# The liquid state divided by DT * DT in a decoder layer woven by a planner

## The chip, the cores and the metric

The kernel runs on one core of a Trainium2 chip, in one launch. Its engines work in parallel, each through its own queue in program order: TensorE (matmuls and transposes, into eight PSUM banks), VectorE, ScalarE (activations), GpSimd (POOL in the profile) and SyncE (SP), which issues the DMAs. They wait for one another through semaphores. The metric is the device time of the launch in microseconds, lower is better.

## The reference

The input is 2 x 1024 tokens of 256 features, and the layer adds three parts to it in turn: causal attention with a liquid cell and a feed-forward net, cross attention to 77 context tokens, and eight parallel trees of 255 nodes. The change touches the liquid cell:

```
b, s, d = x.shape
...
x = x + attn
ctx = attn.reshape(b * s, d)
xs = _ln(x, g1, b1).reshape(b * s, d)
vs = jnp.zeros_like(xs)

def step(carry, _):
    xs, vs = carry
    u = jnp.tanh(ctx @ w_ctx + xs @ w_x + b_inl)
    vn = vs + DT * (u - xs - vs)
    xn_ = xs + DT * vn
    return ((xn_, vn), None)
(xs, vs), _ = jax.lax.scan(step, (xs, vs), None, length=NUM_ITERS)
x = x + xs.reshape(b, s, d)
```

There are eight steps and DT is 0.1.

## The kernel before, in words

The tokens are cut into NTB = 4 blocks of TB = 512, two for each batch. Each block goes through chains of work written as Python generators: `scores` (first norm, queries, keys, values, the rows' maxima), `values` (exponentials and the weighted sums), `opening` (output projection, sum `h0`), `middle` (the liquid cell, the feed-forward net, cross attention, the last norm) and `leaves` (the trees). They run for different blocks at the same time.

**Who sets the order.** A planner, the class `Clock`, weaves these chains while the program is being built. A chain yields what it needs next: an operation (`Op`) with an engine, a cost and its operands; a set of tiles that must be ready for a matmul, with a number of free PSUM banks; or a condition. `weave` (L354) asks every chain for the earliest time at which it can go on by the planner's own costs, adds what going on is worth (a change of TensorE's kind of matmul counts 0.135 to 0.215 in `TURNS`, L99), and takes the least, in tenths of a microsecond; ties go to the chain that is most behind its due time. If a chain yields a list of operations, the planner takes the one that ends first by its costs; in this way a copy out of PSUM goes to ScalarE or VectorE (`evict`, L167). `beside` (L343) sends a piece of work off as a chain of its own and gives back a condition that it is over. The result is one fixed order for each engine; a different cost or one more operation anywhere can give another order from there on. Matmuls come in three kinds: on the full array, on 32 rows (scores of one head; up to four heads go side by side), and into 32 columns (`p,v`). In the profile nearly all planned instructions have the lines of the planner's helpers (L165 matmul, L181 transpose, L197 ScalarE, L207 VectorE, L216 and L218 GpSimd), so groups are told apart by tiles.

**The liquid cell** (`liquid`, L965) keeps features on the partitions: 2 halves (`c`) of 128 partitions by 512 tokens. Two PSUM banks `ps` hold the argument of the tanh for all eight steps and are only added to. With w the velocity over DT, a step is: tanh of `ps` plus `b_ac` into `w` on ScalarE, once per half; `w` plus the remainder `r` on VectorE (in the first step minus `xs`); the matmuls `w_dx` by `w`, where `w_dx` is `w_x` times DT * DT, into `ps`; then on VectorE, for each half, the state `xs = w * DT * DT + xs` and the remainder `r = w * (1 - DT) - xs`. The first matmuls of a block are `w_x` by `xs`. In the profile `xs` is the tile `xn_l`, because the norm that makes it names it so. At the end `add_tokens_first` transposes `xs` and `add_half` (L652) adds it to `h0` (`h` in the profile).

**Buffers.** Tiles of the middle chain and of the startup come from one ring of six buffers of the same size, with the tag `d`; the seventh tile takes the buffer of an earlier one and has to wait until that one's readers are through. At the start the ring is filled by the loads of `woT`, `w_ctx`, `ctxT`, `xwk`, `xwv` and by the tile `mask32` (L511), which GpSimd fills with the causal mask (a memset and a select). `w_x` (L497) has a buffer of its own.

**The startup.** GpSimd's order is: identity, `mask32`, the constant `half`, then the powers with which the norms take their inverse roots. VectorE's order is: clearing of `qT` and two `nmax`, the cast of `mask32` to `mask` and of the identity, ones for the values, and then the statistics of the first block `xn`, the normalized `xc`. TensorE's order is: `w_ctx` by `woT` (the chain `prepare`, L1198), the first context keys (`ctxT` by `xwk`), the transposes of `xc`, more context keys, the queries. SP issues the loads in the order of the program.

Of the kernel before, what the change touches and what calls it, by code (L numbers as in the profile page):

```python
# [26 lines left out]
DC = D // P  # L27
VROW = H * (HD + 1) + SLOT - HD - 1
FF = 1024
NITER, DT = 8, 0.1  # L30
# [8 lines left out]
_COLS = {}  # L39
# [375 lines left out]
def decoder_kernel(ctx: ExitStack, tc: tile.TileContext, ins: dict, out: bass.AP):  # L415
# [8 lines left out]
    const = ctx.enter_context(tc.tile_pool(name="const", bufs=1))  # L424
# [3 lines left out]
    clock = Clock(nc)  # L428
# [6 lines left out]
    def bank():  # L435
        return banks(1)[0]
# [5 lines left out]
    def dtile(name, shape=(P, DC, TB)):  # L442

        return work.tile(list(shape), F32, tag="d", name=name, bufs=6)


    def load(name, shape, pool=const, tag=None, **kw):
        t = pool.tile([P, *shape], F32, tag=tag or name, name=name + "_sb", **kw)
        flat = t if len(shape) == 1 else t.rearrange("p a b -> p (a b)")
        clock.load(flat, ins[name])  # L450
        return t
# [28 lines left out]
    vecs = load("vecs", (NCOLS,))  # L480
    x0 = load_x(0, "xn")
    d = dict(pool=work, tag="d", bufs=6)
# [11 lines left out]
    xrow = work.tile([P, D], F32, tag="raw", name="xrow", bufs=2)  # L494
    clock.load(xrow, ins["vrows"][0:1, 4 * D :].to_broadcast([P, D]))
    wo = load("wo", (DC, D))
    w_x = load("w_x", (DC, D))  # L497
    xwq = load("xwq", (DC, D))
    xwo = load("xwo", (DC, D))
    paths32 = load("paths", (2, P), pool=work, tag="raw", bufs=2)  # L500
# [1 line left out]
    def col(name, i):  # L502
        at = _COLS[name][0] + i
        return vecs[:, at : at + 1]
# [12 lines left out]

    paths = const.tile([P, 2, P], BF16, tag="paths16", name="paths16")
    w_dx = const.tile([P, DC, D], F32, tag="w_dx", name="w_dx")
    half_b = const.tile([P, 2 * PAR], F32, tag="half_b", name="half_b")  # L520


# [38 lines left out]
    def fill_late():  # L561
        for t in (qT[1], xq, *nmax[2:]):
            yield zeros(t)
        yield clock.vector("tensor_copy", paths, paths32)
        yield clock.activation(w_dx, w_x, AF.Copy, scale=DT * DT)
        for name in ("ff", "trees"):
            for w in streams[name]:
                w.more()
                w.more()
        at = _COLS["b_in"][0]  # L570
        yield clock.vector("tensor_scalar", half_b, vecs[:, at : at + 2 * PAR], 0.5, None, ALU.mult)
        spare.extend(nmax[2:])
        done.add("filled late")
# [37 lines left out]
    def scaled(dst, src, mv, rstd):  # L611

        for i in range(NQ):
# [2 lines left out]
                ALU.subtract, ALU.mult,  # L616
            )

    def evicted(ops, *banks):
        yield ops  # L620
        clock.free(*banks)

    def features_first(dst, src, name, g=None, b=None):

        made = []
        for c in range(DC):
            yield (src,), 1
            ps = bank()
            for i in range(NQ):
                clock.transpose(  # L630
                    ps[:, i * P : (i + 1) * P], src[:, i, c * P : (c + 1) * P], ident
                )
            affine = () if g is None else (col(g, c), col(b, c))
            made.append(clock.beside(evicted(clock.evict(dst[:, c, :], ps, *affine), ps)))
        yield (), lambda: all(m() for m in made)

    def add_tokens_first(dst, src, name):

        made = []
        for j in range(2):  # L640
            yield (src,), 1
            ps = bank()
            for i in range(2):
                for c in range(DC):
                    cols = slice((2 * j + i) * P, (2 * j + i + 1) * P)
                    clock.transpose(
                        ps[:, i * D + c * P : i * D + (c + 1) * P], src[:, c, cols], ident
                    )
            made.append(clock.beside(add_half(dst, j, ps)))
        yield (), lambda: all(m() for m in made)  # L650

    def add_half(dst, j, ps):  # L652

        at = dst[:, 2 * j : 2 * j + 2, :]
        yield clock.vector("tensor_tensor", at, at, ps.rearrange("p (i d) -> p i d", d=D), ALU.add)
        clock.free(ps)

    def project_keys(dst, w, bias, src, n):
# [96 lines left out]
    def norms(tb, x):  # L755

        mv = block[tb]["mv"] = yield from moments(x, f"pre{tb}", "mvx")
        xc = atile(f"xc{tb}", "xn", 2, (P, NQ, D))

        rstd = yield from inverse_root(mv, 1.0 + EPS, EPS * EPS, f"attn{tb}")  # L760
        yield from scaled(xc, x, mv, rstd)
        xn = atile(f"xn{tb}", "xn", 2)
        yield from features_first(xn, xc, f"attn{tb}", "g_attn", "b_attn")
        return xn

    def queries(tb, xn):
# [176 lines left out]
        rstd = yield from inverse_root(mv, 1.0, EPS, name, tag)  # L943
        return mv, rstd

    def layernorm(src, name, g=None, b=None, known=None):

        if known is None:
            known = yield from statistics(src, name)
        xc = dtile(f"xc_{name}", (P, NQ, D))  # L950
        yield from scaled(xc, src, *known)
        dst = dtile(f"xn_{name}")
        yield from features_first(dst, xc, name, g, b)
        return dst

    def add_product(ps, w, src):
        for c in range(DC):
            yield (src[:, c, :],), None
            for oc in range(DC):
                clock.matmul(  # L960
                    ps[oc][:, :], w[:, c, oc * P : (oc + 1) * P], src[:, c, :],
                    start=False, stop=c == DC - 1, skip_group_check=True,
                )

    def liquid(tb, h0, aT):  # L965

        for oc in range(DC):
            yield (aT,), 2 if oc == 0 else None  # L970
            if oc == 0:
                ps = banks(2)
            mm_cols(ps[oc][:, :], w_ac, aT, slice(oc * P, (oc + 1) * P))
        done.add((tb, "o"))
        xs = yield from layernorm(h0, f"l1_{tb}", "g1", "b1", block[tb]["known"])
        yield from add_product(ps, w_x, xs)
        r = dtile(f"r{tb}")
        for it in range(NITER):


            w = dtile(f"w{tb}_{it}")
            for c in range(DC):
                yield clock.activation(w[:, c, :], ps[c][:, :], AF.Tanh, bias=b_ac[:, c : c + 1])
            for c in range(DC):
                if it == 0:
                    yield clock.vector("tensor_tensor", w[:, c, :], w[:, c, :], xs[:, c, :], ALU.subtract)
                else:
                    yield clock.vector("tensor_tensor", w[:, c, :], w[:, c, :], r[:, c, :], ALU.add)
            if it < NITER - 1:
                yield from add_product(ps, w_dx, w)  # L990
            for c in range(DC):
                yield clock.vector("scalar_tensor_tensor", 
                    xs[:, c, :], w[:, c, :], DT * DT, xs[:, c, :], ALU.mult, ALU.add
                )
                if it < NITER - 1:
                    yield clock.vector("scalar_tensor_tensor", 
                        r[:, c, :], w[:, c, :], 1.0 - DT, xs[:, c, :], ALU.mult, ALU.subtract
                    )
        clock.free(*ps)
        yield from add_tokens_first(h0, xs, f"xs{tb}")  # L1000

    def add_chunk(po, src, w, f, n):

# [7 lines left out]
            )  # L1011

    def feed_forward(tb, x, h0):
        hn = yield from layernorm(h0, f"l2_{tb}", "g2", "b2")
        yield clock.vector("tensor_tensor", x, x, h0, ALU.add)
        yield from add_row(x, 2)
        done.add("gelu")
        yield (), lambda: "exp" not in done
        yield (hn,), 2
        po = banks(2)  # L1020
        hidden, step = [], {"used": -1}
        into, outof = streams["ff"]

        def outwards():
            for f in range(2 * NFP):
                yield (), lambda: len(hidden) > f
# [247 lines left out]
    block = [{} for _ in range(NTB)]  # L1274
# [131 lines left out]
```

## Time and profile before

| | us |
|---|---|
| median of 3 runs | 1014.68 |
| lowest and highest | 1011.95, 1016.36 |
| the profiled execution, its own time | 1014.24 |
| span of its instructions | 1012.5 |
| busy: TensorE, VectorE, ScalarE, GpSimd | 962.8, 620.5, 412.5, 82.0 |
| liquid stages of the four blocks, from | 141, 336, 563, 780 |

The profile is of one execution. A line of a group gives the code line, the engine, the operation, output and inputs by the program's names (buffer numbers left out), their shapes and the number of instructions; after the bar the busy time in us and the mean of one in ns; after the second bar the idle time of the engine just ahead of them and what ended it. A line of the timeline gives the start and the duration in us, the same names, and in brackets the idle time before and its releaser. A line of windows gives the stretch, and each engine's busy time in it with the number of instructions. A float32 matmul is two passes and shows as two records. PEld is the loading of weights, beside the matmuls.

### The profile page before, as it was taken

Reading aid. Unit: us, or ns where it says so; the run is one execution under the profiler, and the core shown is the slowest. Engines: PE = TensorE matmul, PEld = TensorE weight load, DVE = VectorE, ACT = ScalarE, POOL = GpSimd, SP = SyncE. Lnnn points to the kernel's source line nnn. Section 1 sums busy time; section 2 is a strip of 40 time slices with the busy share of each in tenths; the row PEclk is TensorE's granted clock in tenths of the full one; section 3 lists DMA queues with packets and bytes.
Section 4 is the critical chain, followed back from the end, with each engine's and each line's share of the span. In section 5 each row is a group of like instructions: output and inputs, shape, how many; then the busy total and the mean of one; then the engine's idle time right before and its main releaser. Section 6 shows DMA issues by size and latency. Waiting matters only on the chain.

```text
span 1012.5 us, 14070 instructions
## 1 busy us (share of the span) xinstructions
PE 962.8 (95%) x5496; PEld 484.2 (48%) x5496; DVE 620.5 (61%) x1345; ACT 412.5 (41%) x695; POOL 82.0 (8%) x161
## 2 busy tenths in 40 slices
PE   6898899999999999999999999999999999999898
PEld 4454443345446445564444434346455446645443
DVE  4757768943534798518766995831466881555444
ACT  5143344523573334425444444542652423353331
POOL 0111100100101002102100101010100000000000
PEclk9799999989999999999999999999999999999999
DMA  8120001002000101022000001102200121101221
GB/s 295 55 64 2 1 7 37 1 21 84 22 2 21 32 10 53 21 82 85 22 11 12 12 21 42 43 21 86 61 12 32 31 84 52 48 27 58 83 62 57
DMA packets 22338, 44.87 MB, mean 44 GB/s; under 512 B 2944, under 2 KB 3328, under 8 KB 22272
## 3 DMA queue, kind: packets, MB, share of 16 engines
q1 hardware_dynamic: 22272, 43.97, 14.0%
q8 instruction: 43, 0.70, 0.3%
q14 instruction: 23, 0.19, 0.1%
HBM read 35.57 MB, written 2.10 MB: 37 GB/s over the span
## 4 chain that ended last, share of the span: by engine, by line
PE 87%; DVE 6%; ACT 4%; DMA 1%; issue 1%; SPq 0%; POOL 0%; ACTq 0%; DVEq 0%
PE bank L165 82%; PE bank L181 5%; ACT p L197 2%; DVE nmax L207 2%; DVE top L207 1%; DVE ta L207 1%; DMA xwk_sb<-in_xwk_dram 1%; ACT xp L197 0%; ACT th L197 0%; DMA xn<-in_xtok_dram 0%; DVE xn_l L207 0%; DVE x L207 0%; ACT ta L197 0%; DVE r L207 0%; DVE xc_l L207 0%
## 5 line engine op out<-in xcount | busy, mean ns | idle before, releaser
L197 ACT ACTIVATE p<-bank 128x512 f32<-128x512 f32 (+1 forms) x320 | 155.4, 556 | 152.8 <-PE bank L165 142.5
L207 DVE TENSOR_REDUCE top<-bank 128x1 f32<-128x512 f32 (+3 forms) x256 | 137.8, 581 | 46.9 <-PE bank L165 46.7
L165 PE MATMUL bank<-kT,qT 32*128 32x512 f32 (+3 forms) x768 | 132.1, 544 | 6.8 <-ACT p L197 4.0
L165 PE MATMUL bank<-qT,kT 32*128 32x512 f32 (+3 forms) x768 | 130.9, 532 | 7.8 <-ACT p L197 3.4
L165 PE MATMUL bank<-ta,trees 128*128 128x512 f32 x256 | 126.2, 601 | 2.7 <-DVE ta L207 2.5
L165 PE MATMUL bank<-xn_t,trees 128*128 128x512 f32 x256 | 126.6, 604 | 0.4 <-ACT p L197 0.2
L207 DVE TENSOR_REDUCE nmax<-bank 128x4 f32<-128x308 f32 (+4 forms) x192 | 83.2, 476 | 39.5 <-PE bank L165 37.0
L165 PE MATMUL bank<-w,w_dx 128*128 128x512 f32 x224 | 102.7, 598 | 1.4 <-DVE w L207 1.4
L207 DVE TENSOR_TENSOR x<-x,bank 128x512 f32<-128x512 f32 x40 | 27.3, 684 | 115.4 <-PE bank L165 115.1
L216 POOL TENSOR_SCALAR_AFFINE_SELECT p<-p 128x256 f32<-128x256 f32 x128 | 56.3, 462 | 399.4 <-ACT p L197 226.1
L197 ACT ACTIVATE th<-bank,half_b 128x512 f32<-128x512 f32 x64 | 44.1, 689 | 100.5 <-PE bank L165 100.5
L197 ACT ACTIVATE w<-bank,b_ac 128x512 f32<-128x512 f32 x64 | 43.9, 688 | 86.9 <-PE bank L165 86.8
L165 PE MATMUL bank<-p,v 128*32 128x512 f32 (+3 forms) x768 | 72.6, 503 | 1.4 <-DVE nmax L207 1.0
L165 PEld LDWEIGHTS bank<-ta,trees 128*128 128x128 f32 x256 | 46.2, 190 | 53.0 <-issue 42.9
L165 PEld LDWEIGHTS bank<-xn_t,trees 128*128 128x128 f32 x256 | 44.7, 190 | 51.6 <-issue 42.2
L165 PEld LDWEIGHTS bank<-qT,kT 32*128 32x128 f32 x768 | 48.0, 187 | 40.6 <-ACT p L197 13.3
L165 PEld LDWEIGHTS bank<-w,w_dx 128*128 128x128 f32 x224 | 41.3, 190 | 53.4 <-issue 41.2
L165 PEld LDWEIGHTS bank<-kT,qT 32*128 32x128 f32 x768 | 43.6, 189 | 48.4 <-ACT p L197 11.6
L165 PE MATMUL bank<-xn_l,ff 128*128 128x512 f32 x128 | 59.7, 594 | 0.0
L165 PE MATMUL bank<-ff,ht 128*128 128x256 f32 x256 | 59.2, 379 | 0.0
L207 DVE SCALAR_TENSOR_TENSOR ta<-ta,th 128x1024 f32<-128x1024 f32 x32 | 39.1, 1221 | 30.0 <-ACT ta L197 30.0
L165 PEld LDWEIGHTS bank<-ff,ht 128*128 128x128 f32 x256 | 48.6, 190 | 16.9 <-issue 11.5
(168 smaller groups left out, 1159.9 us busy)
## 6 DMA issues: line engine op xcount, KB each, us to landing
trees<-in_trees_dram SPq DMA_DIRECT2D x64, 256.0 KB, 2.7
ff<-in_ff_dram SPq DMA_DIRECT2D x32, 256.0 KB, 3.0
xn<-in_xtok_dram SPq DMA_DIRECT2D x4, 512.0 KB, 4.0
qT<-qc SPq DMA_DIRECT2D x16, 128.0 KB, 2.3
kT<-kc SPq DMA_DIRECT2D x16, 128.0 KB, 2.3
kc<-in_xtok_dram SPq DMA_DIRECT2D x4, 512.0 KB, 4.4
x<-in_xtok_dram SPq DMA_DIRECT2D x4, 512.0 KB, 4.0
xq<-xqc SPq DMA_DIRECT2D x16, 128.0 KB, 2.3
```

Source lines behind the costliest of these rows:

```text
L165: return self.nc.tensor.matmul(out, w, x, **kw)
L181: return self.nc.tensor.transpose(out, x, ident)
L197: lambda: self.nc.scalar.activation(out, x, func, bias=bias, scale=scale),
L207: "dve", cost, 0.085, out, args, lambda: getattr(self.nc.vector, name)(out, *args, **kw)
L216: self.nc.gpsimd.affine_select(out=out, in_=args[0], **kw)
```

## The change

The kernel keeps z, the state divided by DT * DT, in place of the state. Then a step adds `w` to z as it is.

- `g1b1` holds the norm's gain and offset divided by DT * DT, made by one small instruction; the norm of the liquid cell takes them, so that it gives z (still the tile `xn_l`). The first matmuls of a block use `w_dx` by z in place of `w_x` by `xs`.
- `w` takes its remainder with a factor: `w = r * DT * DT + w` (in the first step z times minus DT * DT). `r` is kept divided by DT * DT too, and is made from z ahead of the step's update: `r = w * (1 - DT - DT * DT) / (DT * DT) - z`. A condition ahead of it waits, in the planner, until the sums of the step before are placed.
- The sum `z = z + w`, once for each half, is sent off beside the steps, as a list of two operations: on VectorE or on GpSimd, whichever the planner takes to end first.
- `add_half` has a variant that multiplies the transposed z by DT * DT while it adds it to `h0`.
- `w_x` is only needed until `w_dx` is made, and is loaded into the ring `d`.

```diff
--- before.py
+++ after.py
@@ -494,7 +494,7 @@
-    w_x = load("w_x", (DC, D))
+    w_x = load("w_x", (DC, D), **d)
...
@@ -517,6 +517,7 @@
+    g1b1 = const.tile([P, 2 * DC], F32, tag="g1b1", name="g1b1")
...
@@ -563,6 +564,10 @@
         yield clock.activation(w_dx, w_x, AF.Copy, scale=DT * DT)
+        at = _COLS["g1"][0]
+        yield clock.vector(
+            "tensor_scalar", g1b1, vecs[:, at : at + 2 * DC], 1.0 / (DT * DT), None, ALU.mult
+        )
...
+    def once(ops):
+        yield ops
+
...
-    def features_first(dst, src, name, g=None, b=None):
+    def features_first(dst, src, name, affine=None):
...
-            affine = () if g is None else (col(g, c), col(b, c))
-            made.append(clock.beside(evicted(clock.evict(dst[:, c, :], ps, *affine), ps)))
+            scale = affine[c] if affine else ()
+            made.append(clock.beside(evicted(clock.evict(dst[:, c, :], ps, *scale), ps)))
...
-            made.append(clock.beside(add_half(dst, j, ps)))
+            made.append(clock.beside(add_half(dst, j, ps, DT * DT)))
...
-    def add_half(dst, j, ps):
-
-        at = dst[:, 2 * j : 2 * j + 2, :]
-        yield clock.vector("tensor_tensor", at, at, ps.rearrange("p (i d) -> p i d", d=D), ALU.add)
+    def add_half(dst, j, ps, scale=None):
+
+        at, two = dst[:, 2 * j : 2 * j + 2, :], ps.rearrange("p (i d) -> p i d", d=D)
+        if scale is None:
+            yield clock.vector("tensor_tensor", at, at, two, ALU.add)
+        else:
+            yield clock.vector("scalar_tensor_tensor", at, two, scale, at, ALU.mult, ALU.add)
         clock.free(ps)
...
@@ -972,32 +985,39 @@
-        xs = yield from layernorm(h0, f"l1_{tb}", "g1", "b1", block[tb]["known"])
-        yield from add_product(ps, w_x, xs)
-        r = dtile(f"r{tb}")
+        z = yield from layernorm(
+            h0, f"l1_{tb}", [(g1b1[:, c : c + 1], g1b1[:, DC + c : DC + c + 1]) for c in range(DC)],
+            block[tb]["known"],
+        )
+        yield from add_product(ps, w_dx, z)
+        r, kept = dtile(f"r{tb}"), []
         for it in range(NITER):
+
 
 
             w = dtile(f"w{tb}_{it}")
             for c in range(DC):
                 yield clock.activation(w[:, c, :], ps[c][:, :], AF.Tanh, bias=b_ac[:, c : c + 1])
             for c in range(DC):
-                if it == 0:
-                    yield clock.vector("tensor_tensor", w[:, c, :], w[:, c, :], xs[:, c, :], ALU.subtract)
-                else:
-                    yield clock.vector("tensor_tensor", w[:, c, :], w[:, c, :], r[:, c, :], ALU.add)
+                yield clock.vector(
+                    "scalar_tensor_tensor", w[:, c, :], (r if it else z)[:, c, :],
+                    DT * DT if it else -DT * DT, w[:, c, :], ALU.mult, ALU.add,
+                )
             if it < NITER - 1:
                 yield from add_product(ps, w_dx, w)
+            yield (), lambda: all(k() for k in kept)
             for c in range(DC):
-                yield clock.vector("scalar_tensor_tensor", 
-                    xs[:, c, :], w[:, c, :], DT * DT, xs[:, c, :], ALU.mult, ALU.add
-                )
                 if it < NITER - 1:
-                    yield clock.vector("scalar_tensor_tensor", 
-                        r[:, c, :], w[:, c, :], 1.0 - DT, xs[:, c, :], ALU.mult, ALU.subtract
+                    yield clock.vector(
+                        "scalar_tensor_tensor", r[:, c, :], w[:, c, :],
+                        (1.0 - DT - DT * DT) / (DT * DT), z[:, c, :], ALU.mult, ALU.subtract,
                     )
+            for c in range(DC):
+                args = "tensor_tensor", z[:, c, :], z[:, c, :], w[:, c, :], ALU.add
+                kept.append(clock.beside(once([clock.vector(*args), clock.pool(*args)])))
         clock.free(*ps)
-        yield from add_tokens_first(h0, xs, f"xs{tb}")
+        yield (), lambda: all(k() for k in kept)
+        yield from add_tokens_first(h0, z, f"xs{tb}")
```

The calls of `layernorm` and `features_first` elsewhere pass the same gains and offsets as before, in the new form.

More of the change, by code (lines that the diff above doesn't have):

```diff
@@ L762, in norms @@
         xn = atile(f"xn{tb}", "xn", 2)
-        yield from features_first(xn, xc, f"attn{tb}", "g_attn", "b_attn")
+        yield from features_first(
+            xn, xc, f"attn{tb}", [(col("g_attn", c), col("b_attn", c)) for c in range(DC)]
+        )
         return xn
@@ L944, in statistics, with layernorm @@
         return mv, rstd
-    def layernorm(src, name, g=None, b=None, known=None):
+    def layernorm(src, name, affine=None, known=None):
         if known is None:
@@ L952, in layernorm @@
         dst = dtile(f"xn_{name}")
-        yield from features_first(dst, xc, name, g, b)
+        yield from features_first(dst, xc, name, affine)
         return dst
@@ L984, in liquid @@
             for c in range(DC):
-                if it == 0:
-                    yield clock.vector("tensor_tensor", w[:, c, :], w[:, c, :], xs[:, c, :], ALU.subtract)
-                else:
-                    yield clock.vector("tensor_tensor", w[:, c, :], w[:, c, :], r[:, c, :], ALU.add)
+                yield clock.vector(
+                    "scalar_tensor_tensor", w[:, c, :], (r if it else z)[:, c, :],
+                    DT * DT if it else -DT * DT, w[:, c, :], ALU.mult, ALU.add,
+                )
             if it < NITER - 1:
                 yield from add_product(ps, w_dx, w)
+            yield (), lambda: all(k() for k in kept)
             for c in range(DC):
-                yield clock.vector("scalar_tensor_tensor",
-                    xs[:, c, :], w[:, c, :], DT * DT, xs[:, c, :], ALU.mult, ALU.add
-                )
                 if it < NITER - 1:
-                    yield clock.vector("scalar_tensor_tensor",
-                        r[:, c, :], w[:, c, :], 1.0 - DT, xs[:, c, :], ALU.mult, ALU.subtract
-                    )
+                    yield clock.vector(
+                        "scalar_tensor_tensor", r[:, c, :], w[:, c, :],
+                        (1.0 - DT - DT * DT) / (DT * DT), z[:, c, :], ALU.mult, ALU.subtract,
+                    )
+            for c in range(DC):
+                args = "tensor_tensor", z[:, c, :], z[:, c, :], w[:, c, :], ALU.add
+                kept.append(clock.beside(once([clock.vector(*args), clock.pool(*args)])))
         clock.free(*ps)
-        yield from add_tokens_first(h0, xs, f"xs{tb}")
+        yield (), lambda: all(k() for k in kept)
+        yield from add_tokens_first(h0, z, f"xs{tb}")
     def add_chunk(po, src, w, f, n):
@@ L1013, in feed_forward @@
     def feed_forward(tb, x, h0):
-        hn = yield from layernorm(h0, f"l2_{tb}", "g2", "b2")
+        hn = yield from layernorm(h0, f"l2_{tb}", [(col("g2", c), col("b2", c)) for c in range(DC)])
         yield clock.vector("tensor_tensor", x, x, h0, ALU.add)
```

## The prediction

> **What bounds the kernel now.** I read the engine totals first, then the startup in the timeline, then the four stretches in which the liquid steps run, and last the single rows that price the edit.
>
> ```profile
> PE 962.8 (95%) x5496; PEld 484.2 (48%) x5496; DVE 620.5 (61%) x1345; ACT 412.5 (41%) x695; POOL 82.0 (8%) x161
> ```
>
> TensorE is busy for 962.8 of 1012.5 us; VectorE for 61%. Work taken off VectorE is worth only what it takes out of the 49.7 us in which TensorE is idle. By the table of waits TensorE's own idle time is put down to VectorE for 18.7 us (its nine rows added up), to ScalarE for 17.0 us and to DMAs for 8.5 us. The windows of the four liquid stages show how little of that lies there:
>
> ```profile
> core 0: us, PE busy (x) PEld busy (x) DVE busy (x) ACT busy (x) POOL busy (x), PEclk, DMA share, GB/s
> 141.00:186.00 45.00, 43.57 (x200) 18.26 (x198) 38.24 (x64) 20.18 (x36) 3.68 (x8) 1.00 0.09 24
> 336.00:384.00 48.00, 45.91 (x212) 21.59 (x215) 45.68 (x92) 17.71 (x26) 1.82 (x3) 1.00 0.07 23
> 563.00:605.00 42.00, 42.00 (x181) 17.83 (x179) 38.42 (x61) 17.89 (x31) 3.36 (x6) 1.00 0.04 13
> 780.00:820.00 40.00, 40.00 (x102) 18.13 (x101) 33.88 (x52) 15.60 (x23) 0.00 (x0) 1.00 0.09 27
> ```
>
> VectorE is 85 to 95% busy there, yet TensorE is idle for 1.43 + 2.09 + 0 + 0 = 3.5 us: other blocks' matmuls fill the gaps between the steps. The startup is the other place, where the kernel is a chain of single waits (timeline, from 0):
>
> ```profile
> 1.32 0.20 POOL masks.py:29 MEMSET mask<- 128x128 f32 x1
> 1.59 0.29 POOL masks.py:30 TENSOR_SCALAR_AFFINE_SELECT mask<-mask 128x128 f32<-128x128 f32 x1
> ...
> 4.06 0.16 DVE L207 CAST mask<-mask 128x128 bf16<-128x128 f32 x1
> ...
> 5.33 1.41 DVE L207 BATCH_NORM_STATS2 stats_pre<-xn 128x6 f32<-128x256 f32 x4 [0.55 <-DMA xn<-in_xtok_dram]
> ...
> 6.80 3.75 PE L165 MATMUL bank<-w_ctx_sb,woT_sb 128*128 128x256 f32 x8 [6.80 <-DMA w_ctx_sb<-in_w_ctx_dram]
> ...
> 9.02 1.38 DVE L207 TENSOR_SCALAR xc<-xn,mv_pre,rs_attn 128x256 f32<-128x256 f32 x4
> ...
> 12.29 0.64 PE L165 MATMUL bank<-ctxT_sb,xwk_sb 128*128 128x77 f32 x4 [1.73 <-DMA xwk_sb<-in_xwk_dram]
> ...
> 12.76 1.04 PE L181 MATMUL bank<-ident,xc 128*128 128x128 f32 x8
> ```
>
> The mask is long done when VectorE casts it, and `xc` (done at 10.40) waits 2.3 us for TensorE, not the reverse.
>
> [...] two selects that take 407 ns each by their median need 1.40 us here, and the sum on VectorE beside them 0.89 us, against its median of 0.684.
>
> ```profile
> 164.30 1.40 POOL L216 TENSOR_SCALAR_AFFINE_SELECT p<-p 128x256 f32<-128x256 f32 x2 [9.25 <-ACT p L197]
> ...
> 165.36 0.89 DVE L207 SCALAR_TENSOR_TENSOR xn_l<-w,xn_l 128x512 f32<-128x512 f32 x1
> ```
>
> [...] the eight passes at 6.80 take 3.75 us, eight of the same width in the matmuls into `v` at 27.81 take 1.97.
>
> **The change part by part.** Three groups of rows price it:
>
> ```profile
> L207 DVE SCALAR_TENSOR_TENSOR xn_l<-w,xn_l 128x512 f32<-128x512 f32 x64 | 44.3, 697 | 0.0
> L207 DVE SCALAR_TENSOR_TENSOR r<-w,xn_l 128x512 f32<-128x512 f32 x56 | 38.9, 694 | 1.2
> L207 DVE TENSOR_TENSOR w<-w,r 128x512 f32<-128x512 f32 x56 | 37.0, 686 | 7.0 <-ACT w L197 6.8
> ```
>
> *State update.* 64 scaled sums at 697 ns leave VectorE: -44.6 us. In the program order of the changed kernel, as built, 47 plain sums come back to VectorE (47 x 0.686 = +32.2) and 17 go to GpSimd. No row shows such a sum on GpSimd; [...] Queued behind a sum there are the selects of `p`, for which `p,v` matmuls wait, and the powers of the norms: 0 to +2 us on TensorE, taken as 0.
>
> *Step.* `w` becomes a scaled sum, as `r` is: 64 x (0.694 - 0.686) = +0.5 us of VectorE. `r` runs ahead of the state update but behind the last one: [...] Between a step's last matmul and the next one's first, the changed TensorE order has mostly 1 to 3 us of other work, as before. I take 0, bounded by -3.5 (all idle time of those stages) and by the lock below.
>
> *Ends.* The multiplied add into `h` costs 8 x (0.744 - 0.684) = +0.5, the scaled gains one 0.16 us instruction, the evictions that the planner now puts on VectorE two more than before, +1.4. VectorE in all: -44.6 + 32.2 + 0.5 + 0.5 + 0.2 + 1.4 = -9.8 us. Where it is hidden behind a busy TensorE it is worth nothing: 0 to -3.5, I take -0.7. `w_dx` for `w_x` in 16 matmuls: 0, the shapes are the same.
>
> *Planner.* From matmul 657 of 3,486 on, in the middle of the first liquid stage, the TensorE order is another one. Counted in both orders, changes between full-array, 32-row and 32-column matmuls fall from 371 to 352. One costs 0.094 us: a 512-column pass starts 0.429 us after the last, but 0.522 where the kind changes. -19 x 0.094 = -1.8 us. In groups of row matmuls that run side by side the longest one sets the time; their columns add up to 99,036 for 99,701: -665 x 2 passes x 0.838 ns = -1.1 us. Where the waits fall in the new order no view shows: I allow a tenth of the 49.7 us of idle time either way, +-5, and take 0.
>
> *Startup, a cost the edit does not name.* `w_x` moves into the ring `d` of six buffers, ahead of `mask32`. That makes `mask32` the seventh and puts it into the buffer of `woT`: in the changed order the mask's memset waits for TensorE's readers of `woT`, done at 10.55. Behind it on GpSimd stand the select, `half` and the powers; on VectorE everything stands behind the mask's cast. Memset to the select's end is 0.56 us (1.32 to 1.88): 11.15. The cast starts at 11.2; from the cast's start to the last memset's end it is 0.72 us (4.06 to 4.78): statistics at about 12.0 for 5.33, 6.65 later. `xc` ends at 17.05 for 10.40, and its transposes on TensorE start at 17.1 for 12.76, behind context matmuls that end at 12.9. **+4.4 us**, with nothing to hide it: all later work hangs on `xn`. The SP queue keeps its order and needs none of these. The idle gap of 4.2 us may also bring the half clock, [...] so 0 is taken.
>
> *Sum.* Against the profiled execution's own time, 1014.24 us (span 1012.5 and 1.7 around it; 0.4 under the median of 1014.68): +4.4 - 1.8 - 1.1 - 0.7 + 0.5 for the lock = +1.3, **1015.5 us**.
>
> **Rivals.** A difference under 0.5% (5.1 us, below 1009.6 or above 1019.8) is about what a measurement of this kernel cannot tell from none.
>
> *A, they cancel* (0.46): the startup's loss and the planner's saving nearly meet; 1015.5, its own range 1010 to 1020.
>
> *B, VectorE was worth more* (0.24): the second liquid window, at 95% VectorE, speaks for it, as do the 18.7 us of waits on VectorE; the 3.5 us of idle time in the windows speaks against. With -3.5 and the -5 of a kinder order: 1014.2 + 4.4 - 2.9 - 3.5 - 5 = 1007.
>
> *C, the lock decides* (0.26): [...] while `r`, `w` or the trees' `ta` (1.22 us, two SBUF inputs) stands ready in VectorE's full queue, so `w` and the bank releases come late. [...] at 6 it gives 1021.7. Six of the 17 sums lie in the second block, where VectorE has the least room. Against it: the planner chooses GpSimd only where VectorE is late.
>
> *D, the edit does less than it says* (0.04): 47 of 64 sums stay, and a late sum on GpSimd holds `r`; a few steps stretch and the half clock comes on top: about 1020, on the slow side.
>
> **Numbers.** Faster B 0.24, same A 0.46, slower C and D 0.30. The range takes most of B and C: 1006 to 1024.
>
> **What would show it.** `mask`'s memset at 10.6 and `xc`'s transposes near 17.1 show the startup step; transposes still near 12.8 show it wrong. `xn_l<-xn_l,w` rows, 47 at about 0.69 on VectorE [...] price the sums; longer two-input sums beside them are the lock. VectorE near 611 us and TensorE's idle time up by some 4 us fit A. A total outside 1006 to 1024, or waits of TensorE on `w` over 4 us, would show it wrong.

## The result and the profile after

| | before | after |
|---|---|---|
| median, us (4 runs each, on the same chip) | 1013.40 | 1024.58 |
| lowest and highest, us | 1011.95, 1016.36 | 1021.87, 1024.87 |
| after / before, 95% interval | | 1.0102 (1.0077 to 1.0127) |
| the profiled execution, its span, us | 1014.24, 1012.5 | 1024.46, 1022.8 |

The changed kernel is 1.0% slower, about 10 us. The forecast was 1015.5 us with a range up to 1024. One execution among all that follow, of the run idle_read, had a granted clock of 0.556 and took 1631 us, and no ratio contains it. Each engine's busy time after the change, as the share of the span and with the number of instructions:

```profile
PE 960.9 (94%) x5496; PEld 486.8 (48%) x5496; DVE 625.3 (61%) x1331; ACT 411.9 (40%) x693; POOL 112.8 (11%) x178
```

TensorE's work fell by 1.9 us, so it is idle for 61.9 us (1022.8 - 960.9) where it was idle for 49.7. VectorE has 14 instructions fewer and is busy 4.8 us longer, not 9.8 us shorter. So some of its instructions now take longer.

**The startup.** Timeline of the changed kernel from 0, start and duration in us:

```profile
7.65 3.75 PE L165 MATMUL bank<-w_ctx_sb,woT_sb 128*128 128x256 f32 x8 [7.65 <-DMA w_ctx_sb<-in_w_ctx_dram]
...
11.47 0.20 POOL masks.py:29 MEMSET mask<- 128x128 f32 x1 [10.10 <-PE bank L165]
...
12.07 0.23 DVE L207 CAST mask<-mask 128x128 bf16<-128x128 f32 x1 [7.93 <-POOL half L515]
...
16.44 1.38 DVE L207 TENSOR_SCALAR xc<-xn,mv_pre,rs_attn 128x256 f32<-128x256 f32 x4
...
17.00 2.21 PE L181 MATMUL bank<-ident,xc 128*128 128x128 f32 x8 [3.30 <-DVE xc L207]
...
19.00 2.68 PE L165 MATMUL bank<-ctxT_sb,xwk_sb 128*128 128x77 f32 x12
...
23.18 1.05 PE L165 MATMUL bank<-xn,wq_sb 128*128 128x512 f32 x2
```

Two lines of the kernel before, to compare the last two with:

```profile
13.63 1.46 PE L165 MATMUL bank<-ctxT_sb,xwk_sb 128*128 128x77 f32 x12
...
15.80 3.60 PE L165 MATMUL bank<-xn,wq_sb 128*128 128x512 f32 x8
```

The memset of `mask` now waits 10.10 us for TensorE, which reads `woT` until 11.40; it stood at 1.32 before. VectorE stands still ahead of the cast for 7.93 us, and the transposes of `xc` start at 17.00 in place of 12.76. Two more numbers count: the eight transposes take 2.21 us (1.04 before) and the context keys 2.68 (1.46 before). TensorE runs at half rate here. The first queries start at 23.18; before they started at 15.80. The later start (4.2 us) and the half rate (3.1 us) make 7.4 us in these two profiles.

**The liquid cell.** Rows of the groups by form (after the first bar busy time in us and mean in ns), then two lines of the table of TensorE's waits (total us, times, longest):

```profile
L207 DVE SCALAR_TENSOR_TENSOR w<-r,w 128x512 f32<-128x512 f32 x56 | 51.7, 946 | 4.8 <-ACT w L197 4.6
L207 DVE SCALAR_TENSOR_TENSOR r<-w,xn_l 128x512 f32<-128x512 f32 x56 | 36.3, 688 | 0.0
L207 DVE TENSOR_TENSOR xn_l<-xn_l,w 128x512 f32<-128x512 f32 x47 | 32.7, 721 | 0.1
L218 POOL TENSOR_TENSOR xn_l<-xn_l,w 128x512 f32<-128x512 f32 x17 | 28.7, 1692 | 96.4 <-DVE r L207 60.9 <-DVE w L207 22.8 <-PE bank L165 12.8
```

```profile
PE bank L165 <- DVE w L207: 7.3, 8, 2.1
PE bank L181 <- DVE xc L207: 3.3, 1, 3.3
```

The first of the two in the kernel before:

```profile
PE bank L165 <- DVE w L207: 1.4, 2, 0.8
```

`r` is at its old price. `w` costs 946 ns on the mean, and the same form costs 688 as `r`. One by one, 14 of the 56 `w` last over 1 us, and these 14 hold 14.4 us more than the rest would. TensorE's wait for `w` rises from 1.4 to 7.3 us. The sum on GpSimd shows 1692 ns.

The windows of the four liquid stages, moved to where they lie now (block 2 starts its first step at 557 instead of 563, since the order is another):

```profile
core 0: us, PE busy (x) PEld busy (x) DVE busy (x) ACT busy (x) POOL busy (x), PEclk, DMA share, GB/s
147.00:192.00 45.00, 42.67 (x192) 17.80 (x194) 38.06 (x60) 18.55 (x32) 9.52 (x11) 1.00 0.09 24
344.00:393.00 49.00, 45.70 (x193) 21.00 (x192) 46.62 (x87) 19.49 (x30) 15.03 (x12) 1.00 0.07 17
557.00:601.00 44.00, 42.16 (x144) 16.55 (x146) 39.26 (x58) 18.75 (x31) 10.18 (x6) 1.00 0.06 18
783.00:824.00 41.00, 40.62 (x98) 17.67 (x97) 34.42 (x52) 15.86 (x22) 3.26 (x3) 1.00 0.08 26
```

TensorE is idle for 2.33 + 3.30 + 1.84 + 0.38 = 7.85 us in them. At the startup PEclk is no help: for 16 to 24 us it says 1.00 in this profile, and 0.50 in that of sums_dve below, which has the same 2.21 and 2.68 us. The half rate is read from the durations.

### The profile page after: what moved, and what is told of

Same layout as the page of the kernel before. It is cut to its first block, busy times and chain, and to the rows that moved or that the text cites. A ratio compares the mean times of both kernels' runs of the same rounds, so it can differ in the third digit from the quotient of the medians.

```text
span 1022.8 us, 14080 instructions
## 1 busy us (share of the span) xinstructions
PE 960.9 (94%) x5496; PEld 486.8 (48%) x5496; DVE 625.3 (61%) x1331; ACT 411.9 (40%) x693; POOL 112.8 (11%) x178
## 4 chain that ended last, share of the span: by engine, by line
PE 80%; DVE 12%; ACT 3%; issue 3%; DMA 1%; POOL 0%; SPq 0%; ACTq 0%; DVEq 0%; POOLq 0%
PE bank L165 75%; PE bank L181 5%; DVE top L207 3%; DVE nmax L207 2%; ACT p L197 2%; DVE w L207 1%; DVE ta L207 1%; DVE r L207 1%; DMA trees<-in_trees_dram 1%; DVE xn_l L207 0%; ACT ta L197 0%; DMA woT_sb<-in_woT_dram 0%; DVE x L207 0%; ACT xp L197 0%; DVE stats_pre L207 0%
## 5 line engine op out<-in xcount | busy, mean ns | idle before, releaser
L165 PE MATMUL bank<-qT,kT 32*128 32x512 f32 (+3 forms) x768 | 127.5, 524 | 8.7 <-DVE top L207 3.8
```

Of the source, the lines that this page charges most:

```text
L165: return self.nc.tensor.matmul(out, w, x, **kw)
```

## The experiments

Two theories were set against each other. *Startup and lock*: `w_x` in the ring delays the mask, and the 17 sums on GpSimd hold VectorE's `w` (this holding is all that *lock* stands for here). *The order*: the planner's new order of TensorE, or a remainder that waits for a late z, costs the time. To keep the order fixed, most kernels leave the planner's view untouched and exchange only the instruction that is issued at a place. In the traces of own_buffer, sums_dve, own_and_dve, pool_all and idle_read_2 TensorE's records stand in the same sequence as in the changed kernel's. Ratios are to the kernel before, run on the same chip, with 95% intervals; 0.1% is 1.0 us.

| run | ratio | median us |
|---|---|---|
| own_buffer | 1.0034 (1.0021 to 1.0048) | 1019.71 |
| sums_dve | 1.0015 (1.0001 to 1.0029) | 1018.17 |
| own_and_dve | 0.9965 (0.9951 to 0.9979) | 1012.88 |
| own_and_dve_2 | 0.9968 (0.9954 to 0.9983) | 1012.55 |
| before_ring | 1.0067 (1.0045 to 1.0090) | 1022.49 |
| after_again | 1.0078 (1.0051 to 1.0105) | 1024.54 |
| pool_all | 1.0117 (1.0089 to 1.0146) | 1028.77 |
| dve_planned | 1.0262 (1.0210 to 1.0314) | 1042.08 |
| before_remainder | 1.0038 (1.0025 to 1.0051) | 1021.18 |
| idle_read | 1.0075 (1.0054 to 1.0096) | 1024.27 |
| idle_read_2 | 1.0078 (1.0055 to 1.0101) | 1024.77 |
| idle_memset | 0.9981 (0.9965 to 0.9996) | 1013.49 |

### The two suspects undone, one by one and together

own_buffer, the changed kernel with `w_x` back in a buffer of its own:

```diff
-    w_x = load("w_x", (DC, D), **d)
+    w_x = load("w_x", (DC, D))
```

> The changed kernel with w_x back in a buffer of its own, so that mask32 waits for nothing; every engine's order is that of the changed kernel. Startup theory (the late mask costs 7 us at the start, of which all later work hangs): xc's transposes near 12.8 us again, and 7 us less than the changed kernel's 1024.6, about 1017.5. Lock theory (the sums on GpSimd hold the next w; the startup's loss is taken up by slack before the end): transposes early, but at most 2 us less, 1022 to 1025.

sums_dve, the changed kernel with the 17 GpSimd sums issued on VectorE at the same places:

```diff
-                kept.append(clock.beside(once([clock.vector(*args), clock.pool(*args)])))
+                pooled = clock.pool(*args)
+                pooled.issue = lambda a=args: getattr(nc.vector, a[0])(*a[1:])
+                kept.append(clock.beside(once([clock.vector(*args), pooled])))
```

> The changed kernel with the 17 sums z + w that the planner gave to GpSimd issued on VectorE at the same places of the program; the orders of TensorE, ScalarE and SP are untouched, the startup stays late. Lock theory: w<-r,w falls from 946 to about 690 ns, TensorE's waits on w from 7.3 to some 1.5 us, and the total by 5 to 7 us, to about 1018.5. Startup theory: VectorE gets 11.7 us of sums back, nothing is gained, 1023 to 1027.

own_and_dve has both edits, and own_and_dve_2 is the same kernel again.

> Both edits at once, the order of the changed kernel throughout: w_x in its own buffer and all 64 sums on VectorE. If startup and lock are the whole loss, what is left is the planner's new order with its 19 fewer changes of matmul kind: 1010 to 1013, at or under the kernel before (1013.4). Order theory (the new order waits more by itself): still 1016 or more.

> own_and_dve once more, as the base of the two kernels with idle work on GpSimd: 0.995 to 0.998 of the kernel before.

Either edit alone takes back a part: 1.0102 (1.0078 when it was run again, below) falls to 1.0034 and 1.0015. Together they give 0.9965 and 0.9968, faster than either of the two kernels. The differences within the first three runs, which share their runs of before, price the suspects in one and the same TensorE order. GpSimd's sums: 1.0034 - 0.9965 = 0.69%, 7.0 us give or take 2.0. The ring: 1.0015 - 0.9965 = 0.50%, 5.1 us give or take 2.0. What is left, -0.35%, is the rest of the change: -3.5 us. The granted clock does not make these differences: its mean over the runs lies between 0.990 and 0.992 in all three.

The traces say the same. In the startup of own_and_dve_2 (timeline) the mask is early and TensorE at full rate:

```profile
1.32 0.20 POOL masks.py:29 MEMSET mask<- 128x128 f32 x1
...
13.55 1.04 PE L181 MATMUL bank<-ident,xc 128*128 128x128 f32 x8
14.43 1.46 PE L165 MATMUL bank<-ctxT_sb,xwk_sb 128*128 128x77 f32 x12
...
16.59 3.60 PE L165 MATMUL bank<-xn,wq_sb 128*128 128x512 f32 x8
```

From the transposes to the first queries it is 3.0 us here and 6.2 in the changed kernel. Of sums_dve and own_and_dve, which differ only in the buffer, sums_dve is 6.4 us behind from the second norm at 41 us to the end: no later slack takes it back. In the other pair, the changed kernel is 6.9 us behind own_buffer at 41 us and 4.5 at the end, so in these single profiles a part is taken back.

The windows of own_and_dve over the same steps (moved with them) and its rows:

```profile
141.00:186.00 45.00, 43.49 (x200) 18.11 (x202) 38.30 (x66) 20.23 (x36) 4.51 (x8) 1.00 0.09 24
337.00:386.00 49.00, 47.47 (x207) 21.98 (x206) 46.62 (x95) 19.93 (x31) 5.53 (x7) 1.00 0.07 17
548.00:592.00 44.00, 44.00 (x154) 17.34 (x156) 39.07 (x65) 20.99 (x37) 3.24 (x2) 1.00 0.06 19
772.00:813.00 41.00, 41.00 (x99) 18.21 (x98) 34.48 (x55) 15.85 (x22) 0.00 (x0) 1.00 0.08 26
```

```profile
L207 DVE SCALAR_TENSOR_TENSOR w<-r,w 128x512 f32<-128x512 f32 x56 | 38.1, 687 | 5.2 <-ACT w L197 5.2
L207 DVE TENSOR_TENSOR xn_l<-xn_l,w 128x512 f32<-128x512 f32 x47 | 31.0, 685 | 0.0
L1018 DVE TENSOR_TENSOR xn_l<-xn_l,w 128x512 f32<-128x512 f32 x17 | 11.6, 681 | 0.0
```

Its line in the table of TensorE's waits:

```profile
PE bank L165 <- DVE w L207: 1.1, 2, 0.6
```

TensorE's idle time in the four stages is 1.51 + 1.53 = 3.04 us, against 7.85: 4.8 us less. VectorE does the 17 sums as well and is busy no longer in these stretches (158.5 us, added up, against 158.4 in the changed kernel). `w` is back at 687 ns, and TensorE's wait for it at 1.1 us, 6.2 less than in the changed kernel; the 7.0 us of the ratios lie close to that.

Where the time goes is seen in a single step. The changed kernel's timeline in block 0:

```profile
178.49 1.28 DVE L207 SCALAR_TENSOR_TENSOR r<-w,xn_l 128x512 f32<-128x512 f32 x2
...
179.26 1.64 POOL L218 TENSOR_TENSOR xn_l<-xn_l,w 128x512 f32<-128x512 f32 x1 [6.74 <-DVE r L207]
...
179.69 2.36 DVE L207 SCALAR_TENSOR_TENSOR w<-r,w 128x512 f32<-128x512 f32 x2
...
181.51 3.70 PE L165 MATMUL bank<-w,w_dx 128*128 128x512 f32 x8 [0.93 <-DVE w L207]
```

The same step in own_and_dve:

```profile
171.79 1.28 DVE L207 SCALAR_TENSOR_TENSOR r<-w,xn_l 128x512 f32<-128x512 f32 x2
172.99 0.68 DVE L207 SCALAR_TENSOR_TENSOR w<-r,w 128x512 f32<-128x512 f32 x1
173.59 0.69 DVE L1018 TENSOR_TENSOR xn_l<-xn_l,w 128x512 f32<-128x512 f32 x1
...
173.80 3.70 PE L165 MATMUL bank<-w,w_dx 128*128 128x512 f32 x8
...
174.20 0.69 DVE L207 SCALAR_TENSOR_TENSOR w<-r,w 128x512 f32<-128x512 f32 x1
```

In the changed kernel the sum is released by the first half of `r`, while VectorE works on the second half, until 179.77. The sum ends at 180.90, 1.13 us later; `w` has begun in the record but ends at 181.44 (179.69 plus the 1.75 us of that instruction, read singly), 0.54 us after the sum. That is one instruction after the other: a sum held off by `r`, then a `w` held off by the sum. With the sum on VectorE, both `w` and the sum between them are over 1.90 us after the first `w` began (172.99 to 174.89). With the sum on GpSimd the two `w` alone take 2.36 us. The transfer to the idle engine costs VectorE more than the sum does itself: a held `w` is 1.06 us longer (1.75 against 0.69), and a sum takes 0.60 us of VectorE's queue (172.99, 173.59, 174.20). From the end of `r`, TensorE gets its `w` after 1.74 us in the changed kernel and after 0.73 us in own_and_dve.

### The ring alone, in the kernel before

before_ring is the kernel before with `w_x` loaded into the ring (the reverse of the first diff), and after_again the changed kernel again, for its startup.

> The kernel before with one edit, w_x loaded into the ring d; w_x stays in use by the first matmuls of each block, so that its buffer is not given back until the last of them. Every engine's order is that of the kernel before. Startup theory: xc's transposes near 17 us, the first 15 us of TensorE's work at half clock, +5 to +7 us: about 1020. If the loss is taken up later: within 2 us of 1013.4. The ring has one buffer less for the rest, which may add waits of its own (0 to +3).

> The changed kernel once more, unaltered, so that its ratio stands beside those of its variants. From the variants, startup 0.7% and lock 0.9% over own_and_dve's 0.9965: a ratio of 1.010 to 1.012 to the kernel before.

The ring alone makes the kernel before 0.67% slower, 6.8 us give or take 2.3, with no other edit. Not all of this need be the startup: here `w_x` stays in use until the last block's first matmuls, so one of the six buffers is missing for the rest, and whether that adds waits was not tried apart. The changed kernel again came out at 1.0078, a little under the 1.010 that its parts had led to expect; its interval (1.0051 to 1.0105) and that of the first measurement overlap.

Four traces have the late mask (after, after_again, sums_dve, before_ring): their transposes start at 17.00 to 17.27, on the mean 3.7 us after those of the nine other traces that were read (12.76 to 14.05), and in all four it is 6.2 us from there to the first queries. In six of the nine others it is 3.0, in three 4.2 to 5.5. So the half rate costs 3.1 us up to the first queries against an undisturbed start, and in these four it did not vary. It can come with an early mask too: own_and_dve has 4.2 us and the same kernel in own_and_dve_2 3.0.

### More on GpSimd, and none offered

pool_all (own buffer for `w_x`) issues all 64 sums on GpSimd, in the order of the changed kernel; dve_planned (own buffer) offers the planner VectorE alone, which gives another order.

```diff
+                vec = clock.vector(*args)
+                vec.issue = lambda a=args: getattr(nc.gpsimd, a[0])(*a[1:])
+                kept.append(clock.beside(once([vec, clock.pool(*args)])))
```

```diff
+                kept.append(clock.beside(once(clock.vector(*args))))
```

> The changed kernel with w_x in its own buffer and all 64 sums z + w on GpSimd, at the places of the program where they were placed; the orders of TensorE, ScalarE and SP are untouched (own_buffer has 17 on GpSimd, own_and_dve none). Lock theory: about 7 us for 17 sums, so 0.4 us a sum and 25 us for 64, a ratio near 1.02, more where two sums in a row (1.6 us each) hold r as well; w<-r,w well over 1 us in its mean. Relief theory (VectorE is freed of 32 us): at or under own_buffer's 1.0034.

> The changed kernel with w_x in its own buffer, and the sum z + w offered to the planner on VectorE alone, so that the planner makes another order for every engine. No late mask, no sums on GpSimd. Order theory, by the count used in the prediction: 351 changes of matmul kind for 371 of the kernel before, -1.9 us, but the longest of each group of row matmuls add up to 106,409 columns for 99,701, +11.2 us: +9 us, a ratio near 1.009. Edit theory (the edit itself decides, the order is noise): 0.996 as own_and_dve.

Groups by form of pool_all:

```profile
L207 DVE SCALAR_TENSOR_TENSOR w<-r,w 128x512 f32<-128x512 f32 x56 | 83.3, 1520 | 7.3 <-ACT w L197 7.2
L1018 POOL TENSOR_TENSOR xn_l<-xn_l,w 128x512 f32<-128x512 f32 x47 | 75.7, 1624 | 45.1 <-DVE r L207 45.1
...
L218 POOL TENSOR_TENSOR xn_l<-xn_l,w 128x512 f32<-128x512 f32 x17 | 29.4, 1733 | 33.5 <-DVE r L207 33.5
```

Now nearly every `w` is held (49 of 56 over 1 us). The loss grows by 1.0117 - 1.0034 = 0.83%, 8.4 us give or take 3.2 for 47 sums, or 0.18 us each; the first 17 cost 7.0 / 17 = 0.41 each. That is less than the 25 us for 64 that were expected. TensorE's wait for `w` hardly grows, from 7.3 us in own_buffer to 7.8: few of the newly held `w` are ones that TensorE stands waiting for, and per sum the planner's 17 cost the most.

dve_planned is the slowest of all, though it has no sum on GpSimd. Its order has 351 changes of kind, the changed kernel 352, but longer groups of row matmuls: 106,409 columns, by the prediction's price (106,409 - 99,036) x 2 x 0.838 ns = 12.4 us more. In the trace of the kernel before that price is seen so: the four float32 matmuls of `w_ctx` by `woT` leave eight records; 512-column passes start 0.429 us apart by their median, 0.838 ns a column; and a stretch of row matmuls takes what its longest rows take, from its start to the next matmul 1.07 us for four heads of 512 columns and as much for two of 512 beside two of 384 and 128 (medians of 62 and 18 stretches). dve_planned's profiled span, 1033.6 us, is 22.6 over own_and_dve's (1011.0), so the count carries its sign and about half its size; 4.8 us more is a single wait of TensorE for `xc_t` by the table of waits. The rest was not followed further. Its six times fall into two groups, 1035 to 1037 us and 1047 to 1050, the second at a mean granted clock of 0.976 for 0.990, so that the median of 1042.08 belongs to neither; the faster three alone are 1.9% over the kernel before.

### The remainder ahead of the update, alone

before_remainder is the kernel before with only `r = w * (1 - DT - DT * DT) - xs` taken ahead of the state's update, all on VectorE; the planner gives another order.

> The kernel before with one part of the change: the state undivided, but the remainder r made from the old state ahead of its update, r = w * (1 - DT - DT * DT) - xs, both on VectorE. The planner makes another order: 371 changes of matmul kind as before, row groups 100,674 columns for 99,701, +1.6 us. Order theory: a ratio of 1.001 to 1.003. If r taken early is worth something by itself: under 0.998.

It gains nothing: 1.0038. By the count of the orders (371 changes as before, 973 columns more) it should lose 1.6 us; it loses 3.9 give or take 1.3. The part of the change that sounds most like a gain shows none here; apart from the order that comes with it, it was not measured.

### A sum that nobody needs

Two readings were left of why `w` is late beside GpSimd's sums: the two engines' instructions hold each other up (the lock), or the dependence (a late z holds the next `r`). idle_read takes own_and_dve, in which all sums are on VectorE, and issues beside 14 of the 17 a GpSimd sum of `r` and `w_dx` into `w_x`, which is dead by then. Nothing waits for its result; only the next `r`, which is written over the one it reads, has to come after it. idle_memset puts there a four-column sum, which keeps the release by `r` and the reading of it, and three memsets of 512 columns, which read nothing. Both compute the layer in full, with this work added.

```diff
+                        nc.gpsimd.tensor_tensor(idle, r[:, c, :], flat, ALU.add)
```

```diff
+                        nc.gpsimd.tensor_tensor(idle[:, 0:4], r[:, c, 0:4], half, ALU.add)
+                        for _ in range(3):
+                            nc.gpsimd.memset(idle, 0.0)
```

> own_and_dve (all 64 sums on VectorE) with 14 idle sums on GpSimd beside it, at the places where the changed kernel has its sums of steps 1 to 7: each reads r and w_dx (two SBUF inputs, 512 columns) and writes into w_x, which nothing reads any more. Nothing waits for them but the next r in the same tile. The orders of the other engines are untouched. Lock theory: w<-r,w rises to about 900 ns in its mean and 5 to 7 us of the loss come back: a ratio of 1.001 to 1.004. Waiting theory (the loss came from steps that waited for z off GpSimd): as own_and_dve, 0.9965.

> The same 14 places, but each time GpSimd adds four columns of r to a constant (so that it starts when r is there) and then clears w_x three times, some 1.5 us of writing without a read. [...] Lock theory: w<-r,w stays near 690 ns, 0.9965 to 0.998. If any work on GpSimd beside VectorE slows it: as idle_read, 1.001 to 1.004.

> idle_read once more, for a profile at full clock: by its first times a ratio of about 1.0075 to the kernel before, where own_and_dve has 0.9968; by the lock theory w<-r,w near 900 ns in its mean (14 idle sums, up to 1.06 us each on a w of 0.69), and TensorE's waits on w some 5 us longer than without.

idle_read_2 is the same kernel as idle_read, and its profile is the one shown. Groups by form and TensorE's wait for `w`, of idle_read_2:

```profile
L207 DVE SCALAR_TENSOR_TENSOR w<-r,w 128x512 f32<-128x512 f32 x56 | 46.6, 842 | 4.6 <-ACT w L197 4.6
...
L1024 POOL TENSOR_TENSOR w_x_sb<-r,w_dx 128x512 f32<-128x512 f32 x14 | 29.6, 2113 | 73.8 <-DVE r L207 73.7
```

```profile
PE bank L165 <- DVE w L207: 9.7, 11, 1.7
```

And of idle_memset:

```profile
L207 DVE SCALAR_TENSOR_TENSOR w<-r,w 128x512 f32<-128x512 f32 x56 | 38.2, 690 | 5.2 <-ACT w L197 5.2
...
L1025 POOL MEMSET w_x_sb<- 128x512 f32 x42 | 22.3, 532 | 2.4
L1023 POOL TENSOR_TENSOR w_x_sb<-r,half 128x4 f32<-128x4 f32 x14 | 15.4, 1103 | 66.3 <-DVE r L207 66.2
```

```profile
PE bank L165 <- DVE w L207: 1.4, 3, 0.6
```

Fourteen useless sums cost 1.0075 - 0.9968 = 1.07% on the same chip, 11 us give or take 2.6 (1.10% with idle_read_2, on another chip). `w` is at 842 ns and TensorE waits 9.7 us for it. That is more than the 5 to 7 us expected: VectorE still does its own sums here, and those beside the idle ones are held too (885 ns in the row of L1020, for 686). The memsets and small sums keep GpSimd busy longer in the record (37.7 us, the waiting of the small sums included, against 29.6) and cost 0.13%, within the interval, with `w` at 690 ns and TensorE's wait at 1.4 us.

What holds `w` is not a late z, for nothing but the next `r` waits for the idle sums, and not a busy GpSimd: beside 14 sums of 512 columns with two inputs `w` takes 842 ns on the mean, beside 42 memsets of 512 columns and 14 sums of four 690. The step shown above agrees, with 1.13 us and then 0.54 us one behind the other. Whether one wide input on GpSimd would do as two did was not run. By what part of the chip the two engines hold each other up, the traces do not show.

## Where the prediction was right and where it was wrong

The likeliest case, A, did not come: the direction of the result is that of case C. The time lies 0.58 us beyond the range, but the interval of the ratio allows 1021 to 1026, so on which side of 1024 it fell is chance. The prediction's own signs say more: `xc`'s transposes came where it put them, but TensorE waits 7.3 us for `w`, where over 4 was to show it wrong, VectorE is busy for 625 us instead of 611, and TensorE's idle time is up by 12.2 us instead of 4. By the prediction's steps:

| step | predicted, us | measured, us |
|---|---|---|
| startup, delay of the mask | +4.4 | +3.7, from the start of the transposes |
| startup, half rate | 0 | +3.1, to the first queries |
| the lock | +0.5 | +7.0 (2.0 either way) |
| changes of kind, row groups, VectorE's relief | -1.8 - 1.1 - 0.7 = -3.6 | -3.5 and -3.2 (1.4 and 1.5 either way) |
| sum | +1.3 | +10.3 by these terms; +10.3 by the ratio 1.0102, +7.9 by 1.0078 |

The two startup rows are read from traces. By the ratios of the experiments the two together are 5.1 us (2.0 either way), and the sum is then 8.6.

- **The startup's delay was right, worked out from the orders alone.** The memset came at 11.47 for 10.6, since the first loads landed 0.85 us later in that execution, and the transposes at 17.00 for 17.1. They need only the first of the four `xc`, not the last, and that made up for the late memset.
- **The half rate was taken at nothing.** The prediction saw that the idle gap of 4.2 us might bring it and took 0, by an estimate of its author's that no trace shows. In four traces out of four TensorE is idle for 3.30 to 3.68 us just ahead of the transposes, and all four run at half rate from there, for about 6 us or longer, by their durations: eight transposes in 2.21 us for 1.04, twelve context passes in 2.68 for 1.46. In three of them the context passes just ahead of that gap still ran at full rate (0.64 us for four); in the profile of the changed kernel they were at half rate already (1.10 us). Why the half rate came every time was not tested. The prediction counted only the gap behind these passes as idle, but from the last matmul by `woT` to the transposes TensorE has little else to do: 0.64 us of work in 5.6 us in before_ring. With an early mask the pace varies (3.0 to 5.5 us from the transposes to the queries in nine traces), with a late one it did not in four (6.2). The measured loss is 3.1 us.
- **The lock was the step that decided, and it was mis-sized.** A sum on GpSimd takes 1.13 us in the step shown above, from the end of VectorE's `r` to its own, and 1.26 us in the shortest of the 17 records; the row's 1692 ns holds the wait for VectorE's two-input instruction as well (0.51 us of the 1.64 in that step, 179.26 to 179.77). What failed is "Against it: the planner chooses GpSimd only where VectorE is late", and the +0.5 in the sum, for which the prediction shows no working. The planner's costs know nothing of the two engines holding each other up, so to it GpSimd ends first where VectorE has work queued, and in the liquid steps that is the next `w`. For 17 sums 14 `w` were held, by 1.03 us on the mean: of the 14.4 us, about half reached TensorE. Case C put the total at 1021.7 for 6 us of it, and had 0.26.
- **The windows bound only a gain.** That TensorE was idle for only 3.5 us in the liquid stages limits what can be won there, and so the prediction used it. It does not limit a loss: the same stages now have 7.85 us. VectorE at 85 to 95% with a hidden wait is a reserve already used up.
- **Order and relief came out right in their sum**: own_and_dve has no delayed mask, no sum on GpSimd and the same TensorE order, and gives -3.5 us for -3.6. The three terms were not measured apart, and the agreement is in part luck: the count of orders gave 12.4 us where dve_planned's profile shows 22.6, and 1.6 where before_remainder lost 3.9, and VectorE, with all 64 sums, is busy for 618.0 us in own_and_dve, only 2.5 less than before. Less the 11.6 us of the 17 it would be 606.4, a few us below the 610.7 that the prediction's terms give. The changed kernel's 625.3 is lengthened by the lock.
- **B and D.** B's kinder order of -5 us did not come. D needed a sum on GpSimd to hold `r`; `r` stayed at 688 ns with no idle time ahead of it, and a sum that nobody reads costs no less. The half clock that D adds on top did come.

Single profiles of one order differ: own_and_dve is 0.35 us behind own_and_dve_2 at the `r` near 181 us (181.41 for 181.06) and 2.8 us in the span (1011.0 for 1008.2), at a mean granted clock of 0.993 for 0.995. So apart from the startup the sizes above rest on the ratios, and the traces only show where the time lies. before_ring is 7.4 us behind before at the first queries (23.24 for 15.80) and 10.6 in the span (1023.1 for 1012.5). Over all its runs the mean granted clock is 0.986 for 0.990; whether the missing buffer has a part in it stays open. Whether a planner that prices the lock would find an order better than that of own_and_dve was not tried.

## What to carry to other kernels

Before a two-input instruction is given to GpSimd, look at what VectorE runs at that moment: if it is two-input work on the critical path, the offload can cost VectorE more time (1.06 us here) than keeping the instruction (0.60 us), and a planner that takes "whichever ends first" is drawn to these very moments. When a tile moves into a shared ring, count which tile gets the buffer of which: the cost falls on another tile, here a mask that stood at the head of everything. To price one suspect in a planned kernel, exchange the issued instruction and leave the planner's view alone; the order then stays, and the difference is the suspect's.

## What the runs showed of the hardware that was not expected

- GpSimd's 512-column memset (532 ns) beside VectorE's two-input work costs it nothing that can be seen: `w` 690 ns against 692 in own_and_dve_2.
- The wait goes both ways, and a record on GpSimd holds it. The four-column sums of idle_memset last from 199 to 2922 ns, 545 by their median. One that begins at 180.41, while VectorE is in a two-input sum, ends at 182.73, after four two-input instructions of VectorE in a row (the last ends at 182.66), none of which is lengthened. Others get in between `r` and `w`, as the wide sums do in the step above: the one at 175.00 ends at 175.51, 0.06 us after the `r` ahead of it, and the `w` behind it takes 0.68 us. What decides which of the two happens was not found out.
- In pool_all VectorE and GpSimd meet in nearly every step (49 of 56 `w` over 1 us), and yet TensorE's wait for `w` is 7.8 us against 7.3 with 17 sums: most of the added lateness finds slack.
- In all four traces with an idle time of 3.3 to 3.7 us ahead of the transposes these ran at half rate, and the printed clock for 16 to 24 us missed it in one of three (1.00 in after, 0.50 in sums_dve and before_ring); durations of equal passes did not.
